# Moving the depthwise convolutions of six images into the first pass of a two-layer attention kernel

## The chip, the core and the metric

The kernel runs on one core of a Trainium2 chip. A core has a matrix engine (TensorE, in the profile PE for the matmuls and PEld for the weight loads), a vector engine (VectorE, DVE), a scalar engine (ScalarE, ACT), a general engine (GpSimd, POOL) and a queue that issues transfers (SyncE, SP). Each has its own stream of instructions and waits for the others by semaphores. The metric is the time of one execution on the device in microseconds; the times shown are the median, lowest and highest of three runs.

## What is computed

Two layers follow each other on eight images of 32 x 32 positions (1,024 rows) with 512 channels, all in float32.

```python
# layer 0, per image: x is [1024, 512]
xn  = group_norm(x)                          # 32 groups of 16 channels
q, k, v = split(xn @ w_qkv + b_qkv)          # 8 heads of 64
att = softmax((q/8) @ (k/8).T) @ v           # 1024 keys
x   = x + att @ w_out + b_out

# layer 1, per image
hat = layernorm(x)
q   = hat @ wq + bq                                     # 512 channels, 32 x 32
o   = gelu(depthwise_conv(q, dw_w, 7x7, stride 2) + dw_b)  # 512 channels, 16 x 16
off = tanh(o @ pw_w)                                    # two offsets for each of 256 points
smp = bilinear_sample(x, grid + off)                    # 256 rows of 512
kh, vh = smp @ (wv mk_w), smp @ (wv mv_w)
qh  = hat @ (wq mq_w)
z   = softmax(qh @ kh.T) @ vh @ mo_w + mo_b + x         # 256 keys
out = gelu(layernorm(z) @ mlp_w + mlp_b) + z
```

(The products of two weight matrices are formed once, and biases are left out of the listing where they don't matter.)

## The kernel before

The program has two passes, one for each layer, and between them the rows of layer 0's result (`mid`) and their normalized form (`hat_d`) lie in device memory.

The order of the work is written out by hand. `at(place, step)` notes a step under a place, which is a number: its whole part is a unit of the pass, its fraction the position inside the unit. `run_due` issues all steps up to a place. `InOrder` keeps every engine's instructions in the order in which the program issues them, so an instruction that waits holds up all that stands behind it on its engine.

**First pass.** There are 32 units per image, 256 in all: four pairs of heads times eight tiles of 128 queries. `MovedAttention.push` issues a unit: the scores of both heads (`sc`), their maxima on VectorE (`nmax`), the exponentials on ScalarE (`e`), then the steps with a fraction below 0.8, then two block transposes on VectorE (`sq`), and then the rest of the unit's steps. Every second unit, 16 transfers on SP's queue (`et<-sq`) complete the transpose; the product with the values (`av`) runs three units later, one `part` per unit. Between these lie the projections, four matmuls of 512 columns with 128 rows of contraction each (recorded as eight matmul instructions): `qkv_steps` has 24 of them per image, placed by `pair_places`; `out_steps` has eight, placed by `out_places`, and works on the image before: it multiplies by `w_out`, adds the input row block (on GpSimd and VectorE), writes `mid`, normalizes, scales the result on GpSimd (`hat<-hat,lng_row`, `hat<-hat,lnb_row`) and writes `hat_d`. `norm_steps` turns and normalizes the next image. A projection ends in one of three PSUM buffers (`mm`), from which ScalarE or VectorE takes it away. `sc` has two buffers, one for each head of a unit, so the scores of a unit wait for the exponentials of the unit before.

**The depthwise convolution.** It takes the channels in four chunks of 128. A chunk needs two *fills* (`fill`: a projection by `wq`, half of the rows each), two moves into a padded image (`conv_pad`), and 49 *taps* (`conv_tap`): each multiplies a strided window of 16 x 16 by one weight per channel and adds it up. There are two forms of a tap. On VectorE it is one instruction (`SCALAR_TENSOR_TENSOR`). With `part` given, ScalarE multiplies into one of two halves of a small tile, and GpSimd adds that to the sum. In the kernel before, `first_conv` computes image 0 during the last image of the first pass: chunks 0 and 1 by ScalarE with GpSimd, chunks 2 and 3 on VectorE, the last 72 taps behind the end of the attention. Its results lie in `o_first`. All taps of the other seven images (1,372) are on VectorE in the second pass, as many per unit as `conv_counts` says: 40 in each of the first units, 23 to 31 later.

**Second pass.** `prep` forms the products of weights, `points(0)` samples image 0. Then 64 units follow (`unit_steps`), eight per image, each with four tiles of queries for a pair of heads. A unit also holds a quarter of the work behind the attention of the half image before (`back_steps`): `joined` (product with `mo_w`, sum `z`, its statistics), `norm` (`zn`), `turned` (four transposes of `zn` on TensorE), `mlp` and `gelu`. In the order of TensorE, `joined` is at 0.46, a fill at 0.49 (in the units that have one), the first transposes of `e` at 0.56, `turned` at 0.65. `point_steps` and `key_step`/`value_step` sample an image and form its keys and values shortly before its units.

Of the kernel before, what the change touches and what calls it, by code (L numbers as in the profile page):

```python
# [36 lines left out]
PADS = 2  # L37
PADW = W + 6
# [133 lines left out]
class MovedAttention(Attention):  # L172
# [42 lines left out]
    def part(self, et, v, half, first):  # L215
        if half == 0 and first:
            self.av = self.ps_av.tile([P, QB], F32, tag="av", name="av")
        av = self.av[:, ts(half, 2 * P)].rearrange("p (n r q) -> p r n q", n=2, q=SQ)
        for j in range(0 if first else NQT, NQT if first else NT):
            for h in range(2):  # L220
                self.nc.tensor.matmul(
                    av[ds(h * HD, HD)],
                    lhsT=v[:, j, ds(h * HD, HD)],
                    rhs=et[:, h, :, j],
                    start=(j == 0),
                    stop=(j == NT - 1),
                )
# [3 lines left out]
def attention_then_deformable_attention(  # L231
# [126 lines left out]
    o_first = dram.tile([P, NC, NS], F32, tag="o_first", name="o_first")  # L358
# [10 lines left out]
    def conv_tap(acc, pad, dww, cb, u, v, part=None):  # L369

        tap = dww[:, cb, u * KS + v : u * KS + v + 1]
        src = pad[:, ds(u, G, 2), ds(v, G, 2)]
        acc = acc.rearrange("p (i j) -> p i j", j=G)
        first = u == 0 and v == 0
        if part is not None:
            to = acc if first else part().rearrange("p (i j) -> p i j", j=G)
# [9 lines left out]
    with ExitStack() as l0:  # L386
# [4 lines left out]
        NX = 4  # L391
# [3 lines left out]
        def load_x(b, t):  # L395
            if b < B and (b, t) not in xs:
                xs[b, t] = work.tile([P, C], F32, tag="x", name="x", bufs=NX)
                nc.gpsimd.dma_start(xs[b, t], x_tok[b][ts(t, P), :])
# [3 lines left out]
        for t in range(NX):  # L402
            load_x(0, t)
            xs[0, NX + t] = x2[:, t, :]
            nc.sync.dma_start(xs[0, NX + t], x_tok[0][ts(NX + t, P), :])
# [7 lines left out]
        wout = load_w(wp, w_out, "wout")  # L413
# [22 lines left out]
        def norm_steps(b, start, places):  # L436
# [3 lines left out]
            def turn(t):  # L440
# [3 lines left out]
                if t == 0:  # L444
                    room["stats"] = work.tile([P, NC, NT // 2, 6], F32, tag="stats", name="stats")
# [4 lines left out]
                if b > 0 or t < NX:  # L450
                    load_x(b + (t + NX) // NT, (t + NX) % NT)
                    if b == 0:
                        load_x(1, t)
# [60 lines left out]
        def qkv_steps(b, hp, places):  # L514
# [3 lines left out]
            def rows(name, w0, bias, blk):  # L518
                if blk == 0:
# [3 lines left out]
                out = room[name][:, ts(blk, QB)]  # L523
# [6 lines left out]
            def values(t0):  # L530
                if t0 == 0:
                    room["v"] = work.tile([P, NT, P], F32, tag="v", name="v")
# [10 lines left out]
                nc.scalar.copy(room["v"][:, t0 : t0 + 4, :], ps.rearrange("p (t o) -> p t o", o=P))  # L543
# [14 lines left out]
        def out_steps(b, attT, places, last=False):  # L558
# [7 lines left out]
            room = {}  # L566
            to_mid, to_hat = (nc.scalar, nc.gpsimd) if last else (nc.sync, nc.sync)

            def fetch(t):
                room[t] = work.tile([P, C], F32, tag="xr", name="xr", bufs=6)  # L570
# [5 lines left out]
            def out(t):  # L576
                room["ps", t] = project(
                    lambda c: attT[c, t // NQT][:, ts(t % NQT, P)], lambda c: wout[:, c, :]
                )

            def summed(t):
# [3 lines left out]
                stats = work.tile([P, 6], F32, tag="stats", name="stats1", bufs=2)  # L585
# [5 lines left out]
            def norm(t):  # L591
                xr, mv = room[t], room["mv", t]
                hat = work.tile([P, C], F32, tag="hat", name="hat", bufs=3)
# [36 lines left out]
        def first_conv(n):  # L630
# [3 lines left out]
            room = {"pad": {}, "o": {}}  # L634

            def fetch():
                room["w"] = [work.tile([P, C], F32, tag="x", name="wq_x", bufs=NX) for _ in range(NC)]
                for c in range(NC):
                    nc.gpsimd.dma_start(room["w"][c], by_chunk(wq)[:, c, :])
                rest = work.tile([P, NC, QB], F32, tag="xT", name="rest_x", bufs=NX_T)  # L640
                rest = rest.rearrange("p c q -> p (c q)")
                room["bq"] = rest[:, 0:C]
                nc.gpsimd.dma_start(room["bq"], bq.partition_broadcast(P))
                room["dww"] = wp.tile([P, NC, KS * KS], F32, tag="dww_x", name="dww_x")
                nc.gpsimd.dma_start(room["dww"], dw_w.rearrange("(c p) a u v -> p c (a u v)", p=P))
                pad = rest[:, ds(C, PADH * PADW)]
                nc.gpsimd.memset(pad, 0.0)
                pad = pad.rearrange("p (i j) -> p i j", j=PADW)
                part = work.tile([P, C], F32, tag="hat", name="part_x", bufs=3)
                o = work.tile([P, C], F32, tag="hat", name="o_x", bufs=3)  # L650
                room["part"] = part
                for cb in range(2):
                    room["pad"][cb], room["o"][cb] = pad, o[:, ts(cb, NS)]

            def fetch2():
                pads = wp.tile([P, NC, 3 * C], F32, tag="wqkv", name="pads_x")
                o = pads[:, 2, :]
                for i in range(2):
                    pad = pads[:, i, 0 : PADH * PADW]
                    nc.gpsimd.memset(pad, 0.0)  # L660
                    room["pad"][2 + i] = pad.rearrange("p (i j) -> p i j", j=PADW)
                    room["o"][2 + i] = o[:, ts(i, NS)]

            def operand(cb):
                room["hat", cb] = [
                    work.tile([P, C], F32, tag="xr", name="hat_x", bufs=6) for _ in range(2)
                ]
                for par in range(2):
                    nc.sync.dma_start(
                        room["hat", cb][par].rearrange("p (t c) -> p t c", c=P),  # L670
                        hat_d[0][:, ts(par, NC), ts(cb, P)],
                    )

            def fill(cb, par):
                hat = room["hat", cb][par]
                ps = project(lambda c: hat[:, ts(c, P)], lambda c: room["w"][c])
                room["ps", cb, par] = ps

            def fill_end(cb, par):
                conv_pad(room["pad"][cb], room["ps", cb, par], room["bq"], par)  # L680

            def tap(cb, i, part):
                conv_tap(
                    room["o"][cb], room["pad"][cb], room["dww"], cb, i // KS, i % KS,
                    (lambda: room["part"][:, ts(i % 2, NS)]) if part else None,
                )

            def store(cb):
                nc.gpsimd.dma_start(o_first[:, cb, :], room["o"][cb])

            at(n + 10.5, fetch)
            at(n + 24, fetch2)
            taps = KS * KS
            for cb, start in enumerate((12.2, 22.5, 25.2, 27.2)):
                at(n + start - 1.6, lambda cb=cb: operand(cb))
                for par in range(2):
                    at(n + start + par, lambda cb=cb, par=par: fill(cb, par))
                    at(n + start + par + 0.65, lambda cb=cb, par=par: fill_end(cb, par))
                if cb < 2:
                    for i in range(taps):  # L700
                        at(n + start + 1.7 + 0.18 * i, lambda cb=cb, i=i: tap(cb, i, True))
                    at(n + start + 10.7, lambda cb=cb: store(cb))


            for j in range(2 * taps):
                cb, i = divmod(j, taps)
                if j < 10:
                    place = n + 27.9 + 0.4 * j
                elif j < 26:
                    place = last_places(n + per, (j - 10) // 2)[2] + 0.02  # L710
                else:
                    place = n + per + 12
                at(place, lambda cb=cb + 2, i=i: tap(cb, i, False))
            at(n + per + 13, lambda: store(2))
            at(n + per + 13, lambda: store(3))


# [3 lines left out]

        pair_places = [
            (-5.7, -3.7, -1.7, -4.7, -2.7, -0.7),
            (2.3, 5.3, 9.3, 3.3, 10.6, 12.3),
            (13.3, 15.3, 16.3, 14.3, 17.3, 18.3),
            (19.3, 20.3, 21.3, 22.3, 24.3, 25.3),
        ]
        last_pair = (19.3, 20.3, 21.3, 22.3, 23.3, 23.6)
        norm_places = [
            *(18.6, 19.6, 20.6, 21.6, 22.4, 22.5, 23.3, 23.4),  # L730
            *(20.85, 21.86, 22.86, 23.95),
            *(24.9, 24.96, 25.25, 25.85, 26.85),
        ]
        out_places = [0.3, 1.3, 4.3, 6.3, 7.3, 8.3, 10.3, 11.3]
        norm_steps(0, -100, norm_places)

        at(5.4, lambda: add_row(work, bout, wout, bqkv[:, 2 * NC : 3 * NC]))
        qkv_steps(0, 0, (-1, -1, 1.3, -1, 0.3, 2.3))
        run_due(0)
        attT = {}  # L740
        for b in range(B):
            first = b * per
            for hp in range(1, NHP):
                places = pair_places[hp] if b + 1 < B or hp + 1 < NHP else last_pair
                qkv_steps(b, hp, [first + p for p in places])
            if b + 1 < B:
                norm_steps(b + 1, first, norm_places)
                qkv_steps(b + 1, 0, [first + per + p for p in pair_places[0]])
            for hp in range(NHP):
                for qt in range(NT):  # L750
                    n = first + hp * NT + qt
                    if n % per == 0 and b > 0:
# [3 lines left out]
                            [[n + p - 2.5, n + p - 1.4, n + p, int(n + p) + 0.85, n + p + 1.55]  # L756
                             for p in out_places],
                        )
                    if n == B * per - per:
# [485 lines left out]
```

## Time and profile before

| | us |
|---|---|
| median of three runs | 3756.09 |
| lowest, highest | 3749.03, 3759.07 |
| the profiled execution's own time | 3752.78 |
| its span, first to last instruction | 3751.1 |

The profile is of one execution. "Busy" is the time in which an engine executed something. A row of a group gives the engine, the operation, the tiles out<-in, the shapes and the number of instructions, then busy time and mean duration, then the idle time of the engine just before them and what ended it. The granted clock (PEclk) is TensorE's, as a share of full speed; over the whole span it was 0.979. In the trace, the scores of the first unit of the first pass begin at 35.6 us, those of its last unit at 2024.8 us, and those of the first unit of the second pass at 2197.9 us. In the middle of the first pass an image takes 249.9 us.

### The profile page before, as it was taken

What the parts mean: (1) busy time and instruction counts of PE and PEld (TensorE: products, weight loads), DVE (VectorE), ACT (ScalarE), POOL (GpSimd) and SP (SyncE); (2) the same over time, 40 slices, a digit from 0 to 9 for tenths busy, and PEclk for the clock granted to TensorE, in tenths of its full rate; (3) what the DMA queues carried; (4) which work ended last, traced back from release to release, by engine and by line L of the source; (5) the groups of instructions that cost most, each with busy time, mean ns of one, the idle gap of its engine ahead of it and who ended that gap; (6) DMA issues with size and microseconds to landing.
All of it is one profiled execution on the core that took longest, in us unless ns stands there. A gap on an engine that the chain in (4) does not pass through costs nothing.

```text
span 3751.1 us, 46076 instructions
## 1 busy us (share of the span) xinstructions
PE 3561.1 (95%) x16152; PEld 1862.0 (50%) x16152; DVE 2784.0 (74%) x4264; ACT 1528.0 (41%) x3218; POOL 748.9 (20%) x838
## 2 busy tenths in 40 slices
PE   8999999999999999999998877999999999999997
PEld 4554554545545555455453443545555555555443
DVE  5678677776787777767866749898989899998333
ACT  3443443433434434334364122444444444444443
POOL 0003012021030120210445300212121212121212
PEclk9999999999999999999999988999999999999999
DMA  5666666666666666665755411111111111111100
GB/s 154 154 159 186 163 168 174 160 179 162 159 186 163 168 174 162 177 162 148 207 142 149 157 45 45 57 57 57 57 57 57 57 57 57 57 57 35 58 23 31
DMA packets 235350, 438.23 MB, mean 117 GB/s; under 512 B 49296, under 2 KB 53392, under 8 KB 232176
## 3 DMA queue, kind: packets, MB, share of 16 engines
q1 hardware_dynamic: 212528, 363.08, 35.6%
q0 software_dynamic: 21440, 70.11, 5.8%
q8 instruction: 129, 2.11, 0.2%
q10 hardware_dynamic: 1152, 2.10, 0.2%
q14 instruction: 101, 0.83, 0.1%
HBM read 115.84 MB, written 50.86 MB: 44 GB/s over the span
## 4 chain that ended last, share of the span: by engine, by line
PE 73%; DVE 17%; issue 6%; POOL 1%; ACT 1%; DMA 1%; SPq 0%; DVEq 0%; POOLq 0%; ACTq 0%
PE mm L53 45%; PE sc L53 14%; PE av L53 13%; DVE o L53 8%; DVE nmax L53 2%; DVE stats L53 1%; DVE sq L53 1%; ACT e L53 1%; DVE pad L53 1%; POOL mv L53 1%; DVE z L53 1%; DVE smp L53 0%; DMA row<-mid,ii 0%; DVE zn L53 0%; DVE mv L53 0%
## 5 line engine op out<-in xcount | busy, mean ns | idle before, releaser
L53 ACT ACTIVATE e<-sc,nmax 128x1024 f32<-128x1024 f32 (+1 forms) x1024 | 803.6, 798 | 902.7 <-DVE nmax L53 898.8
L53 DVE TENSOR_REDUCE nmax<-sc 128x1 f32<-128x1024 f32 (+1 forms) x640 | 752.8, 1218 | 426.1 <-PE sc L53 425.0
L53 DVE SCALAR_TENSOR_TENSOR o<-pad,dww,o 128x256 f32<-128x256 f32 x1344 | 718.6, 535 | 43.9
L53 DVE STREAM_TRANSPOSE sq<-e 128x1024 f32<-128x1024 f32 x512 | 608.2, 1226 | 50.5 <-ACT e L53 49.3
L53 PE MATMUL sc<-k,q 64*128 64x512 f32 x2048 | 527.3, 618 | 13.5 <-ACT q L53 6.2
L53 PE MATMUL av<-et,v 128*64 128x256 f32 x4096 | 502.8, 388 | 15.9 <-DMA et<-sq 9.0
L53 PE MATMUL mm<-xT,wqkv 128*128 128x512 f32 x1024 | 471.5, 604 | 2.6 <-issue 2.6
L53 PEld LDWEIGHTS av<-et,v 128*64 128x64 f32 x4096 | 275.3, 137 | 321.7 <-issue 177.0
L53 POOL TENSOR_TENSOR mv<-mv,minus_half 128x1 f32<-128x1 f32 x128 | 74.0, 578 | 1409.8 <-DVE mv L53 1341.2
L53 PEld LDWEIGHTS sc<-k,q 64*128 64x128 f32 x2048 | 181.6, 186 | 276.2 <-issue 230.6
L53 PEld LDWEIGHTS mm<-xT,wqkv 128*128 128x128 f32 x1024 | 185.9, 191 | 226.7 <-issue 219.7
L53 ACT COPY et<-mm 128x512 f32<-128x512 f32 x256 | 140.4, 594 | 320.1 <-PE mm L53 319.8
L53 PE MATMUL mm<-wm,zT 128*128 128x512 f32 x512 | 243.4, 619 | 2.9 <-ACT zT L53 2.9
L53 PE MATMUL mm<-wqkv,xT 128*128 128x128 f32 x2048 | 244.5, 278 | 0.0
L53 PEld LDWEIGHTS mm<-wqkv,xT 128*128 128x128 f32 x2048 | 233.8, 192 | 19.9 <-issue 19.9
L53 PE MATMUL mm<-hat_h,wqq 128*128 128x512 f32 x512 | 236.7, 605 | 0.0
L53 PE MATMUL mm<-wo,attH 128*128 128x512 f32 x512 | 231.4, 594 | 3.5 <-DVE attH L53 3.5
L53 PE MATMUL mm<-wout,attT 128*128 128x512 f32 x512 | 233.7, 601 | 0.0
L53 ACT ACTIVATION_READ_ACCUMULATOR e<-sc,nmax 128x1 f32 x1024 | 209.2, 204 | 0.0
L53 PE MATMUL mm<-wq_r,hat 128*128 128x512 f32 x448 | 203.1, 596 | 0.2 <-ACT et L53 0.2
L53 ACT COPY inv<-mm 128x512 f32<-128x512 f32 x128 | 74.3, 580 | 254.1 <-PE mm L53 250.6
L53 PE MATMUL mm<-ident,e 128*128 128x128 f32 x1024 | 149.7, 293 | 16.6 <-DVE z L53 8.2
(153 smaller groups left out, 3625.6 us busy)
## 6 DMA issues: line engine op xcount, KB each, us to landing
et<-sq SPq DMA_DIRECT2D x2048, 128.0 KB, 2.7
xr<-in_x_dram POOLq DMA_DIRECT2D x64, 256.0 KB, 3.8
hat_h<-hat_d SPq DMA_DIRECT2D x16, 1024.0 KB, 5.4
xr<-mid SPq DMA_DIRECT2D x64, 256.0 KB, 2.7
out_dram<-res POOLq DMA_DIRECT2D x64, 256.0 KB, 2.3
x<-in_x_dram POOLq DMA_DIRECT2D x60, 256.0 KB, 4.6
mid<-xr SPq DMA_DIRECT2D x56, 256.0 KB, 2.9
hat_d<-hat SPq DMA_DIRECT2D x56, 256.0 KB, 2.9
```

Of the source, the lines that this page charges most:

```text
L53: return self.tc.keep_in_program_order(op(*args, **kwargs))
```

## The change

Images 0 to 5 (`EARLY = 6`) get their convolutions in the first pass, during the image after them and the one after that: chunk 0 of image b - 1 and chunks 1 to 3 of image b - 2 while image b is in attention. `conv_plan` gives for each chunk the places of its fills and, unit by unit, how many taps ScalarE with GpSimd takes and how many VectorE takes: 34 and 15, 40 and 9, 37 and 12, 35 and 14, in seven or eight units. The two sums (`oa`, `od`) are joined on GpSimd and stored in `o_d`. Images 6 and 7 stay in the second pass, with nine taps per unit, and `conv_load` fetches every image's sums from `o_d`.

The room comes from smaller pools: two input tiles in place of four (`NX`), queries and values in halves (three buffers each), five tiles shared by `xr` and `hat`, and one weight buffer `w` that holds in turn `w_out` and `wq` (`load_weight`, on GpSimd's queue, four times per image). The places of projections, transposes and output steps are shifted to fit, and the pools of the second pass stand in another order.

```diff
+EARLY = 6
...
-                    lhsT=v[:, j, ds(h * HD, HD)],
+                    lhsT=v[not first][:, j % NQT, ds(h * HD, HD)],
...
-    o_first = dram.tile([P, NC, NS], F32, tag="o_first", name="o_first")
+    o_d = [dram.tile([P, NC, NS], F32, tag=f"o{b}", name=f"o_d{b}") for b in range(B)]
...
-        NX = 4
+        NX = 2
...
+        for t in range(NQT):
+            xs[0, t] = work.tile([P, C], F32, tag="attT", name="x0", bufs=NQB * NHP)
+            nc.gpsimd.dma_start(xs[0, t], x_tok[0][ts(t, P), :])
...
-        wout = load_w(wp, w_out, "wout")
+        room_w = {}
...
+        def load_weight(w):
+
+            room_w["w"] = work.tile([P, NC, C], F32, tag="w", name="w", bufs=1)
+            nc.gpsimd.dma_start(room_w["w"], by_chunk(w))
...
+                if name == "q":
+                    out = room[name, blk] = work.tile([P, QB], F32, tag=name, name=name, bufs=3)
...
+                v = work.tile([P, NQT, P], F32, tag="v", name="v", bufs=3)
+                room.setdefault("v", []).append(v)
...
+            def row(name, t):
+
+                k = (t if name == "xr" else NT + t) // NQT
+                if not last or k >= NX_T:
+                    return work.tile([P, C], F32, tag="xr", name=name, bufs=5)
+                if k not in rows:
+                    rows[k] = work.tile([P, NC, QB], F32, tag="xT", name="rows", bufs=NX_T)
+                return rows[k][:, t % NQT, :]
...
-        def first_conv(n):
...
+        def conv_chunk(b, cb, n):
+
+            room = {}
+
+            def operand():
+                room["hat"] = work.tile([P, NT, P], F32, tag="hat_x", name="hat_x", bufs=1)
+                nc.sync.dma_start(room["hat"], hat_d[b][:, :, ts(cb, P)])
+
+            def fill(par):
+                room["ps", par] = project(
+                    lambda c: room["hat"][:, par * NC + c, :], lambda c: room_w["w"][:, c, :]
+                )
...
+            def joined():
+                nc.gpsimd.tensor_tensor(room["oa"], room["od"], room["oa"], ALU.add)
+                nc.gpsimd.dma_start(o_d[b][:, cb, :], room["oa"])
+
+            starts, counts, end = conv_plan[cb]
+            at(n + starts[0] - 2.5, operand)
+            for par, place in enumerate(starts):
+                at(n + place, lambda par=par: fill(par))
+                at(n + int(place) + 0.85 + 0.03 * par, lambda par=par: fill_end(par))
+            i = 0
+            for unit, by_scalar, by_vector in counts:
+                early = by_scalar if unit == end else by_scalar // 2
+
+                for k in range(by_scalar):
+                    place = 0.05 + 0.01 * k if k < early else 0.9 + 0.01 * k
+                    at(n + unit + place, lambda i=i: tap(i, "oa", True))
+                    i += 1
+                for k in range(by_vector):
+                    place = 0.86 + 0.01 * k if unit != end else 0.1 + 0.01 * k
+                    at(n + unit + place, lambda i=i: tap(i, "od", False))
+                    i += 1
...
+        conv_plan = [
+            ((24.3, 25.3),
+             ((26, 3, 2), (27, 4, 2), (28, 6, 3), (29, 6, 3), (30, 6, 2), (31, 6, 2), (32, 3, 1)), 32),
+            ((32.3, 32.6),
+             ((33, 6, 2), (34, 6, 2), (35, 4, 0), (36, 6, 3), (37, 4, 0), (38, 5, 0), (39, 4, 0),
+              (40, 5, 2)), 41),
+            ((41.3, 41.6),
+             ((42, 6, 3), (43, 5, 1), (44, 6, 3), (45, 5, 1), (46, 5, 1), (47, 4, 0), (48, 6, 3)), 49),
+            ((49.3, 49.6),
+             ((50, 6, 2), (51, 6, 3), (52, 6, 3), (53, 5, 2), (54, 4, 1), (55, 4, 1), (56, 4, 2)), 56),
+        ]
...
         pair_places = [
-            (-5.7, -3.7, -1.7, -4.7, -2.7, -0.7),
-            (2.3, 5.3, 9.3, 3.3, 10.6, 12.3),
-            (13.3, 15.3, 16.3, 14.3, 17.3, 18.3),
-            (19.3, 20.3, 21.3, 22.3, 24.3, 25.3),
+            (-5.7, -2.7, -1.7, -3.7, -0.7, 2.3),
+            (4.3, 1.3, 10.3, 6.6, 9.2, 11.6),
+            (12.3, 14.6, 17.2, 13.6, 18.3, 19.3),
+            (20.3, 20.6, 21.3, 22.3, 23.3, 27.3),
         ]
...
         norm_places = [
-            *(18.6, 19.6, 20.6, 21.6, 22.4, 22.5, 23.3, 23.4),
-            *(20.85, 21.86, 22.86, 23.95),
+            *(4.4, 8.4, 12.4, 16.4, 21.4, 22.4, 22.5, 23.4),
+            *(9.85, 17.86, 22.86, 23.95),
             *(24.9, 24.96, 25.25, 25.85, 26.85),
         ]
-        out_places = [0.3, 1.3, 4.3, 6.3, 7.3, 8.3, 10.3, 11.3]
+        out_places = [3.3, 5.3, 6.3, 7.3, 11.3, 13.3, 14.3, 15.3]
...
+                    for place, w in ((0.95, w_out), (7.6, wq), (9.95, w_out), (15.6, wq)):
+                        at(first + place, lambda w=w: load_weight(w))
+                for i, cb in chunks:
+                    if 0 <= i < EARLY:
+                        conv_chunk(i, cb, first - per if cb else first)
...
-        cv, late, late2, first, cvhat, raw, wp = (
-            pool(n) for n in ("cv", "late", "late2", "first", "cvhat", "raw", "w2")
+        first, raw, late, late2, cv, cvhat, wp = (
+            pool(n) for n in ("first", "raw", "late", "late2", "cv", "cvhat", "w2")
...
         def conv_counts():
-            units = [40, 40, 39, 39, 38]
-            units += [19, 26, 27, 27, 32, 32, 33]
-            for _ in range(3, B):
-                units += [25, 13, 25, 31, 26, 28, 23, 25]
-            return units
+            taps = (B - EARLY) * NC * KS * KS
+            return [0, 0] + [9] * (taps // 9) + [taps % 9]
```

## The prediction

> **What bounds the kernel now.** I read the page's shares and slices first, then the busy time by stage, then TensorE's instructions in order of time.
>
> ```profile
> PE 3561.1 (95%) x16152; PEld 1862.0 (50%) x16152; DVE 2784.0 (74%) x4264; ACT 1528.0 (41%) x3218; POOL 748.9 (20%) x838
> ...
> PE   8999999999999999999998877999999999999997
> DVE  5678677776787777767866749898989899998333
> ACT  3443443433434434334364122444444444444443
> POOL 0003012021030120210445300212121212121212
> ```
>
> TensorE (PE) is in use for 95% of the span. VectorE (DVE) is at 6 to 8 tenths in the first pass (slices 1 to 22) and at 8 to 9 in the second, while the convolutions last. ScalarE and GpSimd have room. That invites the change; but the stages must be asked what another microsecond on each engine is worth there.
>
> ```profile
> core 0: us, PE busy (x) PEld busy (x) DVE busy (x) ACT busy (x) POOL busy (x), PEclk, DMA share, GB/s
> 1023.70:1273.60 249.90, 247.25 (x1285) 127.45 (x1284) 184.89 (x220) 103.41 (x176) 45.04 (x49) 1.00 0.64 169
> 2024.80:2197.90 173.10, 138.16 (x472) 75.10 (x472) 93.44 (x181) 34.47 (x70) 69.30 (x79) 0.87 0.47 148
> 2197.90:2613.70 415.80, 366.92 (x1347) 193.85 (x1346) 365.75 (x718) 148.91 (x404) 58.04 (x60) 0.94 0.14 47
> 2800.00:2986.00 186.00, 180.52 (x704) 95.44 (x704) 168.14 (x323) 79.93 (x211) 38.08 (x40) 1.00 0.16 57
> 3620.70:3661.30 40.60, 36.01 (x144) 19.51 (x144) 12.91 (x23) 19.12 (x50) 7.28 (x8) 0.96 0.07 26
> ```
>
> The stretches are: one image of the first pass; the passage between the passes; the first 16 units of the second; one image (eight units) in its middle; two units near its end, without convolution. TensorE's idle time in them is 2.7, 34.9, 48.9, 5.5 and 4.6 us. So VectorE's taps cost time only in the third stretch (40 taps a unit, DVE busy 366 of 416) and at the passage. In the middle, TensorE is as full as in the first pass, although DVE is at 90%.
>
> ```profile
> 849.75 1.99 PE L53 MATMUL sc<-k,q 64*128 64x512 f32 x8
> 851.67 1.95 PE L53 MATMUL av<-et,v 128*64 128x256 f32 x16
> 853.55 3.70 PE L53 MATMUL mm<-wout,attT 128*128 128x512 f32 x8
> 857.08 3.60 PE L53 MATMUL mm<-xT,wqkv 128*128 128x512 f32 x8
> 860.61 1.99 PE L53 MATMUL sc<-k,q 64*128 64x512 f32 x8
> ```
>
> In a unit of the first pass the first two rows recur. With one projection a unit lasts 7.43 us (875.99 to 883.42), with two, as here, 860.61 - 849.75 = 10.86. **A further projection costs 3.43 us.** A fill is a projection.
>
> ```profile
> 3638.49 1.04 PE L53 MATMUL mm<-ident,e 128*128 128x128 f32 x8
> 3641.86 0.33 PE L53 MATMUL mm<-ident,zn 128*128 128x128 f32 x1 [2.33 <-DVE zn L53]
> ```
>
> These are rows from the units without convolution. TensorE has finished the first transposes of `e` and waits 2.3 us for `zn`: sum, statistics, GpSimd's power and normalization follow each other there. In a unit with a fill, the fill stands in this gap. Hence an image without fills and taps isn't 8 x 3.43 = 27.4 us shorter: eight units of 40.6 / 2 = 20.3 and 15 us for keys and values (`smp` by `wvk` and `wvv`: 7.8 and 7.2) make 177.4, against 186.1 with them. Eight fills are worth 8.7 us there, 1.1 each.
>
> **The change part by part**, against the profiled execution's 3752.8 us (the median is 3 us above it).
>
> *Fills.* 48 fills stand in the first pass in place of 8: 8 each during images 2 to 6, two during image 1, and six during the last image, which had 8. The other projections stay. 40 x 3.43 = **+137 us**, all on the path, since TensorE has 2.7 us per image to spare. [...] The row is a distance between starts, not a busy time, so I take it.
>
> *Taps.* Prices come from the taps of image 0:
>
> ```profile
> L53 ACT ACTIVATE part_x<-rest_x,dww_x x96: 512/540/569, 1896.3 to 2054.5; 128x256 f32<-128x256 f32 x96
> L53 POOL TENSOR_TENSOR o_x<-part_x,o_x x96: 717/727/964, 1896.9 to 2055.4; 128x256 f32<-128x256 f32 x96
> ```
>
> and of the second pass:
>
> ```profile
> L53 DVE SCALAR_TENSOR_TENSOR o<-pad,dww,o x1344: 471/485/2969, 2214.5 to 3450.9; 128x256 f32<-128x256 f32 x192
> ```
>
> Per image, 146 taps on ScalarE take 146 x 0.54 = 79 us, 142 additions on GpSimd 142 x 0.73 = 104, four joins and stores about 5, and on VectorE 50 taps x 0.535 (mean of the page) + 8 moves x 0.69 = 32. Added to 103, 45 and 185 busy that is 182, 154 and 217 of some 284 us: none becomes the bound on average. They cost something unit by unit. I added up each unit of the new plan from the rows (scores 1.92, product 1.88, projection 3.43 to 3.77, maxima 2 x 1.22, block transposes 2 x 1.23, GpSimd's output additions 1.27 each). Three kinds of unit have another engine above TensorE. Units 8 and 16 hold no projection now: TensorE 4.3 us, VectorE 6.5 and 7.0; before, only one unit was without (5.37 us, 0.6 above its TensorE work). That is +4.3. Units 4 and 12 have six taps beside three output additions and a power: GpSimd 9.4 against 7.9, of which half may be caught up in the next unit, +1.5. Units 24 and 26 exceed by 0.9 and 0.7. Together about 7.3 per image, 36 for five images. During image 1 three units lack a projection (+4), during the last image nine in place of three (+10). Sum **+50 us**. It may be 5, if waits overlap well, or 150, if the queues hold each other up.
>
> What hides the rest: scores of the next unit need ScalarE's second exponential, which ends about 1.6 us before TensorE's projection does. ScalarE idles 99.8 us per 32 units for `nmax`, VectorE 46.6 for `sc`, so 3.1 and 1.5 us per unit. A third late tap on ScalarE waits for the addition two before it, and behind it stand the next exponentials; where GpSimd is busy with `hat`, that can take the cover away.
>
> [...] But between 1940 and 2040 us, with GpSimd half busy, taps took 522 ns on average against a median of 485: 2 us per image. I take the trace.
>
> *Transfers and queues.* Four loads of 1 MB per image on GpSimd's queue, into one buffer. Each issue waits for TensorE's last use and holds GpSimd's additions, but that use is in the same unit. Nearest rows: 1 MB lands in 5.4 us in the quiet second pass, in 11.9 behind two others. The shortest lead, 9.95 to 11.3, is a unit of 7.6 and 3.8 of the next: 11.4. I take 0; the other end is about 3 us per image, 15 in all, and a gain is excluded, as the weight was resident. `hat_x` on SP's queue delays the `et` moves by an issue of 0.9; one set of moves is issued from 818.39 to 829.15, lands by 831.9 and is needed at 836.7, so 4.8 us cover it. Two input tiles for four: 4.5 us to landing, at least one unit ahead; 0. Start: 0, within 5 either way. The new order of pools is counted in the next line.
>
> *Passage.* TensorE waits 9.0 us for the last `et`: SP's queue stood behind a store (`mid`) that ScalarE issued late, behind taps. It waits 9.0 and 1.7 us for `wq_r` and `mk_w`, whose place was still in use; in the new order they lie in room that is free after the last projection. Two fills (7.0) before the first unit go. **-27 us**. The 8.6 us wait for the first samples stays.
>
> *First 16 units.* From 415.8 to 16 x 20.3 + 22 (keys and values of one and a half images) + 7 (two bias rows) + 6 (five fills at 1.2) = 360: **-55 us**.
>
> *Units 16 to 51.* Four and a half images, 841 us now: 4.5 x 177.4 + 11 fills x 1.1 = 810: **-31 us**. Nine taps, 5 us of VectorE, lie in gaps of 6 us each. From unit 52 on nothing changes.
>
> Sum: 137 + 50 - 27 - 55 - 31 = +74: 3827 for the profiled execution, **3830** for the median. TensorE gets in the first pass what it had nearly free in the second; what is late next in the second pass is `zn`.
>
> **The rivals.** (1) The likeliest, as above, 0.58: 3830, by itself 3800 to 3870. (2) The queues interlock well, as in the last image before, where 5.5 taps per unit left units at 7.4 to 7.6 us: only some 5 us of stalls, 3785; 0.20. Against it: no output steps shared GpSimd then. (3) ScalarE holds up the exponentials in all 78 or so units with six taps. If each loses 1.2 us beyond the 1.6 of cover: +94, 3924; 0.16. (4) Faster: [...] With a fill at 0 it is 3830 - 137 = 3693; it decides from (27 + 55 + 31 - 50) / 40 = 1.6 us per fill downwards. [...] against it 3.43 us; 0.06. That the change doesn't do what it says has nothing for it: the plan's counts add up to 49 for each chunk.
>
> **How the numbers follow.** About 0.3% (11 us) can be told from no change. Faster is (4), 0.06. Within 0.3%, 3745 to 3767, is the low edge of (2), 0.04. Slower is the rest, 0.90. The range, 3770 to 3910, takes in (1), most of (2) and the low part of (3); it leaves out (4), the edge of (2) and the upper half of (3).
>
> **What would show it.** An image in the middle of the first pass at 283 to 286 us, TensorE idle there for 7 to 12; units with a fill about 3.4 us longer per fill; units 8 and 16 at 6 to 7 us. The first unit of the second pass at about 2198 + 137 + 50 - 27 = 2358; `zn` ending a wait of 2.3 us in most units after it; the first 16 units at 360. I am wrong if images of the first pass last under 270 (rival 4), or if ScalarE's `e` ends long waits of TensorE there (rival 3), or if second-pass units without fill fall under 20 us.

## The result and the profile after

| | before | after |
|---|---|---|
| median, us | 3755.26 | 3872.77 |
| lowest, highest | 3749.03, 3759.07 | 3871.95, 3874.32 |
| profiled execution, span | 3752.78, 3751.1 | 3871.95, 3870.2 |

The ratio after to before is 1.0315, with a 95% interval of 1.0297 to 1.0333: the change costs 117.5 us. The forecast was 3830, 43 us less. The page of the kernel after, first its shares of busy time, then its slices:

```profile
PE 3607.8 (93%) x16152; PEld 1884.1 (49%) x16152; DVE 2496.4 (65%) x3486; ACT 1894.8 (49%) x3996; POOL 1378.5 (36%) x1667
...
PE   7999989989989989989999989999999999999897
...
DVE  5777767868768778777776872466565656542333
ACT  3443355655555555565564541444454444444442
POOL 1002146536536536646645633022131212122212
```

The taps have moved as planned: GpSimd has 630 us more work than before, ScalarE 367 more, VectorE 288 less. TensorE has the same 16,152 matmuls. In the first pass it was full before; now an 8 recurs in every third slice.

The busy time by stage, in the columns shown for the kernel before. The stretches are an image in the middle of the first pass, the passage, the first 16 units of the second pass, and its units 16 to 51:

```profile
core 0: us, PE busy (x) PEld busy (x) DVE busy (x) ACT busy (x) POOL busy (x), PEclk, DMA share, GB/s
1130.40:1427.50 297.10, 281.35 (x1351) 141.43 (x1350) 228.37 (x279) 171.77 (x323) 161.60 (x204) 0.97 0.60 165
2291.60:2439.60 148.00, 131.98 (x460) 73.23 (x458) 42.79 (x89) 23.62 (x53) 44.44 (x47) 0.88 0.53 163
2439.60:2761.10 321.50, 303.75 (x1234) 165.86 (x1234) 189.89 (x351) 149.47 (x405) 58.88 (x62) 0.97 0.15 52
2761.10:3567.10 806.00, 747.62 (x2953) 408.32 (x2952) 444.21 (x793) 363.36 (x947) 168.69 (x182) 0.97 0.15 52
```

An image of the first pass takes 297 us where 283 to 286 were forecast, and TensorE idles 15.8 us in it. No other engine is near full: the next, VectorE, is busy for 228 of the 297 us. So TensorE must be waiting for something that isn't an engine's capacity. All its longer waits of the whole span, largest first (total, times, longest):

```profile
PE mm L54 <- DVE zn L54: 102.1, 46, 6.2
PE mm L54 <- DMA hat_x<-hat_d: 69.2, 6, 13.1
PE mm L54 <- DVE mv L54: 23.9, 8, 7.5
PE sc L54 <- ACT e L54: 17.3, 26, 1.7
```

The first row is the second pass, and was forecast. The second is not in the forecast: six waits of 11 to 13 us, one per image, for the fetch of the rows that the fills read. TensorE's instructions in order of time, around the start of such an image:

```profile
1130.42 1.99 PE L54 MATMUL sc<-k,q 64*128 64x512 f32 x8
1132.34 1.95 PE L54 MATMUL av<-et,v 128*64 128x256 f32 x16
1145.36 9.88 PE L54 MATMUL mm<-w,hat_x 128*128 128x512 f32 x16 [11.08 <-DMA hat_x<-hat_d]
1155.17 1.99 PE L54 MATMUL sc<-k,q 64*128 64x512 f32 x8
```

and what SP's queue issued in that time:

```profile
1085.61 54.34 SPq L54 DMA_DIRECT2D et<-sq  x64
1139.99 0.60 SPq L54 DMA_DIRECT2D hat_x<-hat_d  x1
1162.12 3.23 SPq L54 DMA_DIRECT2D et<-sq  x5
```

The unit starts at 1130.42 and holds both fills of chunk 1. Its operand is fetched only at 1139.99, inside the same unit, behind the 16 `et` moves of the unit before, which are still being issued then (16 of them take 10.4 us, by a row shown below; the row of 64 merges four such sets, with pauses of some 4 us between them). The fills begin 5.4 us after the fetch is issued, and the unit lasts 24.8 us, where two projections take 10.86.

Why so late? The fetch is noted at `first fill - 2.5`. But chunks 1 to 3 of image b - 2 are noted only when image b begins, with `first - per`. For chunk 1 that place is 32.3 - 2.5 - 32 = -2.2: it lies two units in the past when it is noted. `run_due` issues it at the next opportunity, which is in the image's first unit. Chunks 2 and 3 have their fetch at +6.8 and +14.8 and are in time, as is chunk 0 (21.8).

By stage, from the starts of the units' first scores (us):

| | before | after | forecast change | measured change |
|---|---|---|---|---|
| start, image 0 | 274.2 | 278.0 | 0 | +3.9 |
| image 1 | 249.8 | 258.9 | +11 | +9.1 |
| images 2 to 6, each | 249.9 | 296.9 | +34.7 | +47.1 |
| last image, to its last unit | 251.4 | 270.0 | +3 | +18.6 |
| passage | 173.1 | 148.0 | -27 | -25.1 |
| units 0 to 15 of the second pass | 415.8 | 321.5 | -55 | -94.3 |
| units 16 to 51 | 835.9 | 806.0 | -31 | -29.8 |
| units 52 to the end | 301.5 | 303.0 | 0 | +1.5 |

These add up to the difference of the spans, 119.1.

### The profile page after: what moved, and what is told of

Same layout as the page of the kernel before. It is cut to its first block, busy times and chain, and to the rows that moved or that the text cites. A ratio compares the mean times of both kernels' runs of the same rounds, so it can differ in the third digit from the quotient of the medians.

```text
span 3870.2 us, 47305 instructions
## 1 busy us (share of the span) xinstructions
PE 3607.8 (93%) x16152; PEld 1884.1 (49%) x16152; DVE 2496.4 (65%) x3486; ACT 1894.8 (49%) x3996; POOL 1378.5 (36%) x1667
## 5 line engine op out<-in xcount | busy, mean ns | idle before, releaser
L54 POOL TENSOR_TENSOR oa<-part_x,oa 128x256 f32<-128x256 f32 x852 | 646.1, 758 | 607.3 <-ACT part_x L54 561.7
L54 PE MATMUL sc<-k,q 64*128 64x512 f32 x2048 | 552.3, 625 | 19.3 <-ACT e L54 17.3
L54 ACT ACTIVATE part_x<-pad_x,dww_x 128x256 f32<-128x256 f32 x852 | 438.1, 543 | 237.6 <-POOL oa L54 235.3
L54 DVE SCALAR_TENSOR_TENSOR chunk<-pad,dww,chunk 128x256 f32<-128x256 f32 x384 | 255.5, 665 | 9.9
L54 PE MATMUL mm<-wm,zT 128*128 128x512 f32 x512 | 251.7, 637 | 2.9 <-ACT zT L54 2.9
L54 PE MATMUL mm<-w,hat_x 128*128 128x512 f32 x384 | 185.9, 638 | 69.2 <-DMA hat_x<-hat_d 69.2
L54 PEld LDWEIGHTS mm<-wqkv,xT 128*128 128x128 f32 x2048 | 234.2, 192 | 20.3 <-issue 18.9
L54 PE MATMUL mm<-w,attT 128*128 128x512 f32 x512 | 234.0, 602 | 0.0
L54 DVE SCALAR_TENSOR_TENSOR od<-pad_x,dww_x,od 128x256 f32<-128x256 f32 x276 | 219.5, 795 | 5.5
```

The costliest lines, as they stand in the source:

```text
L54: return self.tc.keep_in_program_order(op(*args, **kwargs))
```

## The experiments

**The fetch alone.** If the late fetch is the unforeseen part, noting all four chunks of image b - 1 one image earlier takes it away and leaves all else.

```diff
-chunks = [(b - 2, cb) for cb in range(1, NC)] + [(b - 1, 0)]
+chunks = [(b - 1, cb) for cb in range(NC)]
...
-conv_chunk(i, cb, first - per if cb else first)
+conv_chunk(i, cb, first)
```

> The changed kernel with one thing mended: the fetch of chunk 1's operand (hat_x) is noted an image earlier, so that it is issued at its planned place, 2.5 units ahead of the fills, and not at the start of the fills' own unit. Theory: TensorE's wait of 11.1 us for hat_x at the start of six images is only this late issue; 13.4 us per image with what follows go, 6 x 13.4 = 80, so 3785 to 3800 us, and unit 0 of an image falls from 24.8 to 11 us. Rival: SP's queue is full there (64 moves of et stand end to end), so an earlier fetch makes the et moves late instead, TensorE waits for et, and the time stays at 3840 to 3873.

Measured: 3783.39 (3782.75 to 3785.99), ratio to before 1.0083 (1.0066 to 1.0100), 89 us less than after. The same place in this kernel, first TensorE, then SP's queue:

```profile
1102.27 1.99 PE L54 MATMUL sc<-k,q 64*128 64x512 f32 x8
1104.18 1.95 PE L54 MATMUL av<-et,v 128*64 128x256 f32 x16
1106.06 7.13 PE L54 MATMUL mm<-w,hat_x 128*128 128x512 f32 x16
```

```profile
1059.40 37.72 SPq L54 DMA_DIRECT2D et<-sq  x45
1097.17 0.60 SPq L54 DMA_DIRECT2D hat_x<-hat_d  x1
1101.40 10.38 SPq L54 DMA_DIRECT2D et<-sq  x16
```

The fetch goes out 8.9 us ahead of the fills, the unit lasts 10.86, and no wait for `hat_x` is left. Images 2 to 6 take 282.6 to 283.2 us. The 89 us split in two: TensorE's idle time falls by 67.0 (its waits for `hat_x` were 69.2), and its busy time by 22.1, though it does the same work. The rows show where most of that comes from: 16 matmuls took 9.88 us after the wait and take 7.13 here. After all six waits they took 57.2 us (8.73 to 9.88 each), 14.5 more than six times 7.13 (the clock is taken up below). By stage, 83 of the 89 us are in the first pass. The other 6 are in the passage, and are not shown to come from the fetch: TensorE idles no less there (17.7 us, 16.0 in the kernel after), but the same matmuls run at a mean clock of 0.93 in place of 0.88. What is left, +30 us against the kernel before in the same series (3753.01), is what the change costs with its fetch in time. The further edits start from this kernel, except where it is told.

**The price of a fill in the first pass.** Half of the fills there are left out: the second half of each chunk's padded image is written from the first fill.

```diff
-conv_pad(conv["pad"], room["ps", par], conv["bq"], par)
+conv_pad(conv["pad"], room["ps", 0], conv["bq"], par)
...
-                at(n + place, lambda par=par: fill(par))
+                if par == 0:
+                    at(n + place, lambda par=par: fill(par))
```

> As e1_operand, with the second fill of every first-pass chunk left out (both halves of the padded image are written from the first fill): 24 projections fewer, all taps and moves stay. Theory: TensorE is full in the first pass and a projection costs 3.43 us, so 24 x 3.43 = 82 us less than e1_operand, about 3709. Rival: [...] at most 20 us less.

Measured in one run: 3704.41, so 79 us less for 24 fills, 3.3 each; 75 of them lie before the second pass, which makes 3.1 each. Images 2 to 6 fall to 269.0 to 272.0 us, some 12 less for four fills. Three of the four save 3.43 us each (unit 0 goes from 10.86 to 7.43). The fourth, in unit 25, leaves that unit without a projection, and the units around it lose part of the gain again. So the distance between starts, 3.43, was the right price, and 79 us are far above the 20 of the rival.

**The price of the taps.** Each chunk keeps one tap of either kind; fills, moves, joins and stores stay. 852 taps of ScalarE with GpSimd and 276 of VectorE are left out.

```diff
-            i = 0
+            i, seen = 0, set()
...
                 for k in range(by_scalar):
+                    if i > 0:
+                        i += 1
+                        continue
...
                 for k in range(by_vector):
+                    if 'od' in seen:
+                        i += 1
+                        continue
+                    seen.add('od')
```

> As e1_operand, but of every first-pass chunk only the first tap on ScalarE and the first on VectorE are computed; fills, moves, joins and stores stay. Theory: taps lie beside TensorE's work; what they cost is the stalls of a few units, between 282.6 us per image now and the 277.3 that fills alone make, part of which is units 8 and 16 without a projection and stays: 15 to 30 us less than e1_operand in all, 3755 to 3768. Rival: ScalarE's wait for GpSimd's additions holds up the exponentials in most units with six taps, about 1 us in each: 60 to 90 us less, about 3710.

Measured in one run: 3751.53, 32 us less; 27 of them lie before the second pass. One image in the columns shown above, first with all taps (the first experiment's kernel), then with few:

```profile
1102.30:1385.40 283.10, 278.42 (x1349) 140.37 (x1348) 228.39 (x279) 171.68 (x323) 161.50 (x204) 0.99 0.62 173
```

```profile
1091.97:1370.68 278.71, 275.75 (x1350) 139.89 (x1349) 191.07 (x232) 105.34 (x180) 53.55 (x61) 1.00 0.62 176
```

GpSimd loses 108 us of work in an image, ScalarE 66, VectorE 37, and the image becomes 4.4 us shorter. Per unit: units 24 and 25 together lose 3.0, units 5 and 6 lose 1.0 each; 4 and 12 don't move. Units 8 and 9 stay at 20.4 to 21.0 us together without the taps, so those two are slow for another reason.

**Fewer images.** Images 2 to 5 go back to the second pass, at 25 taps per unit.

```diff
-EARLY = 6
+EARLY = 2
...
-return [0, 0] + [9] * (taps // 9) + [taps % 9]
+return [0, 0] + [25] * (taps // 25) + [taps % 25]
```

(and the weight swaps end with the last image that needs them)

> As e1_operand, with two images instead of six in the first pass (EARLY = 2) and 25 taps per unit in the second from unit 2 on. Theory: a fill costs 3.43 us in the first pass and 1.1 in the second, where it fills the wait for zn, as long as VectorE isn't the bound. Four images of the first pass fall from 283 to about 253 (-120), the second pass gains 7 us per image for six images and 21 in units 2 and 3, where VectorE's taps outlast TensorE: 3725 to 3745, below both kernels. Rival: a fill costs the same in both passes, and only the shorter first units of the second pass were gained: about 3790 or more, like e1_operand.

Measured: 3763.03 (3755.50 to 3766.86), ratio to before 1.0022 (1.0015 to 1.0030). A miss: it was to be below before. Fills are cheaper in the second pass, that part holds: it lasts 1507.7 us against 1430.7, while four images of the first pass lose 24 to 25 each. But images 4 to 6 stop at 257.9 to 259.0, not at the 253 that was expected. The shifted places of the other projections now leave units with none: units 0 and 1 of such an image, with one projection between them, last 4.6 + 8.55 = 13.15 us, where TensorE's work is 7.43 + (7.43 - 3.43) = 11.43. Units 8 and 9, and 16 and 17, lose 2.7 and 2.2 in the same way. These three pairs make 6.6 of the 9 us by which image 4 is longer than in the kernel before. Units 24 and 25 hold no projection either; they were not taken apart. The cost of 25 taps a unit in the second pass was sized too low as well: +77 instead of +63.

**The order of the pools.** The second pass's pools stand as before the change.

```diff
-        first, raw, late, late2, cv, cvhat, wp = (
-            pool(n) for n in ("first", "raw", "late", "late2", "cv", "cvhat", "w2")
+        cv, late, late2, first, cvhat, raw, wp = (
+            pool(n) for n in ("cv", "late", "late2", "first", "cvhat", "raw", "w2")
```

> As e1_operand, with the second pass's pools in the order of the kernel before. Theory: of the passage's shorter time, the waits for wq_r and mk_w (9.0 and 1.7 us) were ended by the new order, since wq_r and raw now lie where wqkv was, so they come back: about 3794. Rival: they were held only by the last taps and the late stores behind them, which are gone anyway: 3780 to 3786.

Measured: 3786.91 (3785.30 to 3791.36), ratio to before 1.0095: 3.5 over the first experiment, with overlapping intervals. That is between the two expectations. The profile shows the waits that the theory named, this one above all (for `mk_w` it is 0.7):

```profile
L54 SPq DMA_DIRECT2D wq_r<-in_L_conv_wq_dram x1: 392/392/392, 2258.9 to 2258.9; - x1
...
  DMA wq_r<-in_L_conv_wq_dram: 5.7, 1
```

In the old order `wq_r` is fetched at 2258.9 (2235.3 in the new one), and TensorE waits 5.7 us for it. The passage is 10.4 us longer than in the first experiment, but that is not the price of the order. Here are the passages of the first experiment, of this kernel, and of the last experiment below, which has the new order:

```profile
2208.40:2350.40 142.00, 124.26 (x460) 69.09 (x458) 42.64 (x89) 23.86 (x53) 44.43 (x47) 0.93 0.55 170
2208.00:2360.30 152.30, 132.51 (x458) 73.48 (x456) 41.53 (x89) 23.88 (x51) 44.40 (x47) 0.88 0.50 159
2190.00:2339.90 149.90, 131.48 (x458) 74.43 (x456) 42.91 (x89) 23.94 (x53) 44.32 (x47) 0.87 0.52 161
```

TensorE idles 17.7, 19.8 and 18.4 us in them. So the old order adds 2 us of idle time against the first experiment: other waits shrink where this one is added. The other 8 us are the same matmuls at a lower clock, and with the new order the clock and the length vary as much. The second pass was 4.8 us shorter in this execution; why stays open. So the wait for `wq_r` is shown to depend on the order of the pools; a gain in the total is not shown.

**The gap before `zn`.** The forecast named `zn` as what is late next. TensorE waits for it 2.3 us in each unit with no fill in the gap. The query projection of the next unit needs nothing from this one, so it can stand there.

```diff
-at(n + 0.17, lambda: query_step(*divmod(n + 1, NHP)))
+at(n + (0.17 if n < NHP else 0.5), lambda: query_step(*divmod(n + 1, NHP)))
```

> As e1_operand, with the projection of the next queries in the second pass (query_step) moved from place 0.17 to 0.5, behind the product with mo_w, so that it stands in TensorE's wait for zn. Theory: that wait, 2.3 us in each unit without a fill, is what keeps the second pass from gaining by the fills' leaving; some 40 units lose 2.3 us, every fourth unit gains 1 us for its first product, in all 60 to 90 us less than e1_operand, 3700 to 3730. Rival: another wait takes its place (the transposes of e, or zn later by as much): within 20 us of e1_operand.

Measured in one run: 3663.09, 120 us less than the first experiment; 60 to 90 were expected. Two stretches of the second pass, with the projection where it was (first fence) and in the gap:

```profile
2652.50:3000.00 347.50, 324.69 (x1272) 176.27 (x1271) 209.85 (x373) 158.13 (x416) 76.18 (x82) 0.97 0.17 58
3400.00:3600.00 200.00, 181.06 (x723) 100.05 (x722) 66.06 (x129) 89.68 (x235) 38.28 (x41) 0.96 0.13 44
```

```profile
2652.50:3000.00 347.50, 338.92 (x1366) 181.85 (x1366) 223.74 (x393) 166.93 (x444) 82.79 (x89) 0.99 0.17 61
3400.00:3600.00 200.00, 199.41 (x845) 107.95 (x843) 76.64 (x149) 100.42 (x269) 46.05 (x50) 1.00 0.13 44
```

In the same time TensorE gets 94 and 122 more matmuls done. A unit without other work falls from 19.5 to 17.2 us, and the waits for `zn` from 102.1 to 3.2. Waits of another kind take a small part of its place (for `rs`, the reciprocals of the sums of exponentials, 14.1). That is less than 120. The rest is the clock: of the 119.7 us of span, 84.4 are idle time of TensorE and 35.3 are busy time, with the same matmuls at a mean clock of 0.989 in place of 0.979. What follows one wait for `zn` is seen in small stretches around it in the first experiment, with PEclk in the third column from the right:

```profile
3446.50:3447.50 1.00, 1.00 (x9) 0.80 (x7) 0.69 (x1) 0.30 (x1) 0.00 (x0) 1.00 0.72 275
3447.50:3449.80 2.30, 0.04 (x1) 0.00 (x0) 1.56 (x5) 0.77 (x2) 0.55 (x1) 1.00 0.33 114
3449.87:3451.40 1.53, 1.53 (x12) 1.53 (x13) 0.49 (x2) 0.83 (x2) 0.00 (x0) 0.89 0.00 0
3451.40:3453.00 1.60, 1.60 (x3) 0.67 (x3) 0.00 (x0) 0.83 (x2) 0.00 (x0) 0.50 0.00 0
3453.00:3454.50 1.50, 1.50 (x3) 0.66 (x2) 0.00 (x0) 0.00 (x0) 0.00 (x0) 0.51 0.00 0
3454.50:3456.40 1.90, 1.90 (x6) 0.74 (x5) 0.00 (x0) 0.00 (x0) 0.00 (x0) 1.00 0.00 0
```

TensorE idles for 2.3 us; behind that the granted clock is 0.89 for 1.5 us and 0.50 to 0.51 for 3.1 us, and the eight matmuls `mm<-wm,zT` that follow take 5.12 us here and 3.69 where there was no wait. Not every wait is followed by it: in the kernel after, 20 of the 46 waits for `zn` are followed by eight that take 3.67 to 3.76 us, and 26 by eight that take 3.90 to 5.13; the 18 groups with no such wait take 3.69 or 3.70. In the last experiment's kernel, with the query projection in the gap, at least 60 of these groups take 3.67 to 3.70.

**The same move in the kernel before.** This asks whether the gap was there to be had without the change.

> The kernel before with query_step moved from 0.17 to 0.5 in the second pass, as in e3_query_gap, and nothing else. Theory: fills already fill most of the wait for zn in images 2 to 6, so it gains less than the 120 us that it brought to the changed kernel: about 2.5 us in each of the last 12 units and 3 to 6 us per image before, the first units stay bound by VectorE's 40 taps: 3695 to 3725. Then closing the gap and moving the convolutions go together (e3_query_gap 3663). Rival: it brings as much here as there, 3630 to 3640, and the move of the convolutions is worth nothing with it either.

The edit is that of the experiment above. Measured: 3718.08 (3715.81 to 3722.24), ratio to before 0.9912 (0.9896 to 0.9929), 33 us less. Only the last 12 or so units gain (17.2 us). The units with convolution don't: 186 us for eight, as before. A fill stands in their gap already, and VectorE is 90% busy there; which of the two holds them was not tried. So with the gap filled, the change (with its fetch in time) gives 3663 (one run) against 3718, -55 us; without that, it costs 30.

**The best found.** The query move, with two projections moved: units 8 and 16 had none and now have one; units 9 and 17 had three, fills included, and now have two.

```diff
-(4.3, 1.3, 10.3, 6.6, 9.2, 11.6)
+(4.3, 1.3, 10.3, 6.6, 8.3, 11.6)
...
-(12.3, 14.6, 17.2, 13.6, 18.3, 19.3)
+(12.3, 14.6, 16.3, 13.6, 18.3, 19.3)
```

> e3_query_gap with two projections of the first pass moved from the crowded units 9 and 17 to the empty units 8 and 16 (9.2 to 8.3, 17.2 to 16.3). Theory: units 8 and 9 take 4.9 + 15.4 us where TensorE's work is 19.0, and 16 and 17 likewise; 1.3 us for each pair and image, in seven images about 15 to 18 less than e3_query_gap: 3645 to 3650. Rival: the exponentials and GpSimd's additions bound those units, so only the place of the wait moves: 3658 to 3668.

Measured: 3644.88 (3635.53 to 3648.94), ratio to before 0.9706 (0.9688 to 0.9724). Units 8 and 9 take 7.86 + 10.86 = 18.7 us in place of 4.90 + 15.42 = 20.3, units 16 and 17 as much less; an image takes 279.9 us. TensorE's share, as the first line of the page has it:

```profile
PE 3542.0 (97%) x16152; PEld 1845.4 (51%) x16152; DVE 2494.1 (68%) x3486; ACT 1880.0 (52%) x3996; POOL 1378.6 (38%) x1667
```

This version beats both kernels.

## Why the prediction was right and wrong

The direction and its mechanism were right: work that TensorE had nearly free in the second pass was put into a pass in which TensorE is full. The size came near by luck, through two large errors of opposite sign. Against the forecast of 3827 for the profiled execution, the first pass came out 79 us longer, units 0 to 15 of the second pass 39 shorter, and the rest 5 longer. With its fetch in time the change costs 30 us and not 74. And had units 0 to 15 come out as forecast, the measured time would have been about 3912, just above the range of 3770 to 3910.

- **The step that failed is the one on `hat_x` in *Transfers and queues*: "so 4.8 us cover it".** It asked only what the fetch does to the `et` moves, and not when the fetch itself is issued and whether it lands before its fills. With that went the remark that a change which doesn't do what it says "has nothing for it": the counts of taps were added up, the moment at which chunks are noted was not. The first experiment shows 83 us for this in the first pass (13.3 to 14.0 in each of five images and the last one). The weight loads, which were taken at 0, end none of TensorE's longer waits.
- **Fills, +137: right.** 3.1 to 3.4 each by the second experiment. Rival 4, with a fill at 0, falls; no row spoke for it.
- **Stalls, +50: right as a sum, less so in its places.** With the fetch in time an image is 33 us longer than before, where 34.7 was forecast; the last unit of the first pass starts 184 us later, where 187 was. Units 8 and 16 were given +4.3, and filling them gained 3.3 with their neighbours (last experiment). They lasted only 4.9 us, not 6 to 7: the time came out one unit later. Units 4 and 12 cost nothing (1.5 forecast), the pair at 24 costs 3.0 (1.6 forecast for 24 and 26), and 5 and 6 cost 2.0 that were not seen.
- **VectorE's taps beside GpSimd: "2 us per image" was wrong in size.** VectorE's taps in the first pass, from the page of the kernel after, with GpSimd's additions:

```profile
L54 POOL TENSOR_TENSOR oa<-part_x,oa 128x256 f32<-128x256 f32 x852 | 646.1, 758 | 607.3 <-ACT part_x L54 561.7
...
L54 DVE SCALAR_TENSOR_TENSOR od<-pad_x,dww_x,od 128x256 f32<-128x256 f32 x276 | 219.5, 795 | 5.5
```

  A tap takes 795 ns on average, against the median of 485 before and the 522 that was taken. That is 0.31 x 50 = 15.5 us per image, not 2. The trace that was taken held nine taps between 1940 and 2040 us, and only two of them began while an addition had more than 0.15 us to run; in the kernel after, 153 of the 276 taps began beside an operation of GpSimd with that much to run (see the last section). Yet it cost little time: leaving out nearly all taps makes an image 4.4 us shorter, this included.
- **Passage, -27: right as a sum** (-25.1), but two of its items failed and cancel. From TensorE's waits in the kernel after:

```profile
PE av L54 <- DMA et<-sq: 10.1, 5, 5.0
PE mm L54 <- DVE smp L54: 2.5, 1, 2.5
```

  The wait for the last `et`, 9.0 before, was to go and is still 5.0. The wait for the first samples (`smp`), 8.6 before, was to stay and is 2.5. The waits for `wq_r` and `mk_w` are gone, and so are the two fills. Among the kernels with the new order and the fetch in time the passage lasts 142 to 150 us, mostly with the clock (0.93 and 0.87, with 17.7 and 18.4 us of idle time), so agreement within 2 us says little.
- **The first 16 units, -55: this term was mis-sized.** It charged 20.3 us to all 16. Units 0 to 3 have no work behind the attention of an earlier half image to do, and take 19.6, 13.2, 9.8 and 9.8: 29 us of the 39. The rest is in units 4 to 15 and was not taken apart.
- **Units 16 to 51, -31: right in the time reached** (806, where 810 was forecast). The 841 us that it took for the kernel before are 835.9 in the trace, so its own working gives -26, and -29.8 was measured. What is late next is right as well: `zn` ends 46 waits.
- **The rivals.** Rival 3, exponentials held up by ScalarE's taps, falls: TensorE's waits for `e` are 17.3 us in all, and leaving out nearly all taps gains 32 us, not 94. Rival 2 (5 us of stalls) is not met either: without the late fetch the first pass is 47 us longer than the fills alone make it.

## What to carry to other kernels

A move from one stage to another has two prices: what the work costs at its new place, and what it covered at its old one. Here a fill cost 3.1 to 3.4 us in the full pass and, by an estimate from the rows of the kernel before, 1.1 in the gap of another; putting other independent work into that gap turned the move from a loss of 30 us into a gain of 55. And a step noted under a place is not yet issued there: look up the issue time of each new transfer in the trace, and compare it with its first use.

## What the runs showed of the hardware

**After some of its waits TensorE runs at half the clock.** After an idle stretch of 11.08 us, the granted clock was 0.50 for the next 5 us (here the row for the kernel after, right behind the wait for `hat_x`), and the 16 matmuls of the fills took 9.88 us, 2.75 more than without the wait.

```profile
1145.36:1150.30 4.94, 4.94 (x6) 2.19 (x7) 0.00 (x0) 0.00 (x0) 0.00 (x0) 0.50 0.00 0
```

In the second pass a wait of 2.3 us was followed by a clock of 0.50 to 0.51 for 3.1 us, in the small stretches shown above. Why 26 of the 46 waits for `zn` are followed by slower matmuls and 20 are not, no run here shows. With other work put into the gap, 35 of the 120 us gained were busy time, at a mean clock of 0.989 in place of 0.979.

**A tap on VectorE that begins beside an operation of GpSimd mostly ends just after it.** In the kernel after, where GpSimd is busy for 54% of an image of the first pass, a first-pass tap on VectorE takes 795 ns on average, against 478 with no work of GpSimd beside it (24 taps). One tap that meets an addition, and one that doesn't:

```profile
1318.63 0.73 POOL L54 TENSOR_TENSOR oa<-part_x,oa 128x256 f32<-128x256 f32 x1
1318.74 0.90 DVE L54 SCALAR_TENSOR_TENSOR od<-pad_x,dww_x,od 128x256 f32<-128x256 f32 x1
1366.95 0.47 DVE L54 SCALAR_TENSOR_TENSOR od<-pad_x,dww_x,od 128x256 f32<-128x256 f32 x1
```

The addition ends at 1319.36 and the tap at 1319.64, 0.28 us later. It is so with nearly all: of the 276 taps, 153 begin while such an operation of GpSimd has more than 0.15 us to run, and 149 of these end 0.28 to 0.31 us after it does, also behind six operations on `hat`, which take 1.26 to 1.47 us. (The other four meet GpSimd's power on a single column, of 0.80 us; they take 0.48 and end 0.01 before it.) The longer time is the tap's recorded time, 0.90 us against 0.47 in the rows above, so it counts as busy there.
